# One indirect transfer for all experts' table entries, later loads of the sums' weights and tables, and products of constants at the start, in a conditioned mixture-of-experts layer

## The chip, the core and the metric

The kernel runs on one core of a Trainium2 chip. The metric is the device time in microseconds; the time before is the median of three runs. A profile is one further execution, taken with the hardware profiler, and its rows are in microseconds from the start of its span.

## The reference

For x of 8 x 256 x 1024 (2048 tokens), each of the 8 batches has its own 1024 x 1024 matrix, picked by a number in `itok`; its product with x is the input of a feed-forward layer, whose result is added to x. All in float32.

```
h      = einsum("bsi,boi->bso", x, weight[itok])
g, u   = split(h @ shared_w_gate_up.T);   shared = silu(g) * u @ shared_w_down.T
probs  = softmax(h @ gate_w.T);           two best of 16 experts, their weights scaled to sum 1
g, u   = split(h @ w_gate_up[e].T);       out_e  = silu(g) * u @ w_down[e].T
result = x + shared + sum over the two experts of weight * out_e
```

The condition matrices are loaded by an index that is known at run time alone, and so are the experts' rows.

## The kernel before

**Products in three parts.** Every float32 operand is split into a high part (a cast on ACT, L80) and a low part (a subtraction on DVE, L81), and each product is three matmuls (`mm3`, L103): high by high, high by low, low by high. `load_w` (L89) loads one tile of 128 x 1024 (512 KB) from SP's queue into one of 4 staging buffers `st`, and splits it into one of 5 buffers `hl`. A load can be issued only when the split that used its staging buffer is done; a split can begin only when PE has finished with its `hl` buffer.

**Work between loads.** `between` is a list of small works: `load_w` takes one after each of its splits and asks that it is issued after that split (`tc.issue_after`). Otherwise a planner, which estimates times, sets the order of each engine's instructions; `issue_after` holds a step back behind another. On each engine the instructions run in the order that results.

**Stages.** `cond(b)` computes the condition product of one batch: 8 tiles of weights `wc`, 2 tiles of `xT`, 96 matmuls of 128x512, and two stores of rows to `y_d`. `itok` comes by the very first transfer, and SP reads its number (L211) before it can issue a `wc` load. `route(g)` (L236) computes the gate for one of 4 groups of 512 tokens, picks the two experts on DVE, and writes each token's number and weight to `tab_d` by 8 indirect scatters from POOL (L333). `tab_d` has `SLOTS` places for each expert. `Up` computes the first shared matrices by a scheme of sums and differences of quarter matrices: `stage_a`, `stage_b`, `stage_c`, `stage_d`, each for units u = 0 to 3. `sums_b(u)` loads three tiles (`a11`, `a21` into spare places in `S` and `raw`, `a22` into a staging buffer), and DVE forms three sums of them (L443 to L445), which are split (`shl`), used, and stored in `ss_d` for the second half of the tokens; `sums_d(u)` loads two and forms one (L456). `shared_down(g)` is the second shared matrix, 8 tiles of `sd` for 512 tokens; DVE adds its results from PSUM into `acc` (L554), and SP stores them (L555). There are 7 PSUM banks that take turns.

**Order of the whole.** The main part (L725 to L761) interleaves the eight `cond` with `route` and the stages of `Up` for the first two groups. `tables` (L155) loads the gate's weights and fills `tab_d`; it stands in `between` for `cond(2)`. After `route(3)` a chain of small DVE operations (L778 to L817) sorts the experts by their number of tokens; `order` holds the expert at each place, and its capacity is from `CAPS`.

**Entries.** `entries(pool, ns)` (L660) reads the tables of the experts at places `ns`. For each it issues two transfers from SP, after reading the expert's number: `tb` (the same entries 32 to a row) and `cr` (one row an expert). `places` transposes `tb` on DVE (L676) and makes row numbers `ix` of them on POOL (`segments`, 4 instructions); `weights` transposes `cr`'s weights on PE (L683) and copies them to `cw`. It is called for places 0 and 1 before `shared_down(0)`, with `weights` in `between`, and for 2 to 15 before `shared_down(1)`, with both in `between`. `expert_rows(n)` gathers an expert's rows from `y_d` by 8 to 10 indirect transfers from POOL (L579), in 4 buffers `yg` and one `yl`, and DVE transposes them (L178). After `shared_down(1)` the 16 experts follow, then the shared part of the other two groups, and last `shared_down(2)` and `shared_down(3)`, which store to `out`.

Of the kernel before, what the change touches and what calls it, by code (L numbers as in the profile page):

```python
# [9 lines left out]
F32 = mybir.dt.float32  # L10
# [10 lines left out]
E, I, SI = 16, 256, 1024  # L21
NA = 8
NC = H // P
G = 4
GT = T // G
NB = GT // P

CAPS = (304, 296, 288, 288, 280, 280, 272, 272, 264, 264, 264, 256, 256, 256, 256, 256)
CAP = max(CAPS)
MAIN = 2 * P  # L30
SLOTS = T + CAP
ROW0 = [sum(CAPS[:n]) for n in range(E + 1)]
ZROW = ROW0[E]
PAD = 4 * T
# [3 lines left out]
def adapter_moe_kernel(ctx: ExitStack, tc: tile.TileContext, xT, x, itok, wc, gate, wgu, wd, sgu, sd, out):  # L38
# [43 lines left out]

    last_load = [None]

    homes, loads, last_gather, marks = [whl], [0], [None], []

    between = []

    def load_w(src, parts=1):  # L89
        st = wst.tile([P, 1024], F32, tag="wst", name="st")  # L90
        loads[0] += 1
        hl = homes[loads[0] % len(homes)].tile([P, 2, 1024], FR, tag="whl", name="hl")
        for i in range(parts):
            cs = slice(i * 1024 // parts, (i + 1) * 1024 // parts)
            last_load[0] = nc.sync.dma_start(st[:, cs], src[:, cs])
            end = split(hl[:, 0, cs], hl[:, 1, cs], st[:, cs])
        work = between.pop(0) if between else None
        if work:
            with tc.issue_after(end):
                work()  # L100
        return hl

    def mm3(ps, lhs, rhs, first, last):  # L103
        nc.tensor.matmul(ps, lhs[0], rhs[0], start=first, stop=False)  # L104
        nc.tensor.matmul(ps, lhs[0], rhs[1], start=False, stop=False)  # L105
        nc.tensor.matmul(ps, lhs[1], rhs[0], start=False, stop=last)  # L106


    cpool.tile([P, 96], F32, tag="cpad", name="cpad")
    at3 = [cpool.tile([P, 2, P], FR, tag=f"at3{k}", name=f"at3{k}") for k in range(2)]  # L110
    gpk = cpool.tile([P, NC * 2 * E + P], FR, tag="gpk", name="gpk")
    tri = cpool.tile([P, P], BF, tag="tri", name="tri")
    ones = cpool.tile([P, P], BF, tag="ones", name="ones")
    it_sb = cpool.tile([1, B], I32, tag="it_sb", name="it_sb")
    nc.sync.dma_start(it_sb, itok)

    ident = cpool.tile([2 * E, 2 * E], F32, tag="ident", name="ident")

# [13 lines left out]
    def constants(ring):  # L132
        make_identity(nc, ident)
        tri_f = ring.tile([P, 1024], F32, tag="op", name="tri_f")
        make_upper_triangular(nc, tri_f[:, :P], val=1.0, diag=False)
        nc.vector.tensor_copy(tri, tri_f[:, :P])
        nc.gpsimd.memset(ones, 1.0)
# [69 lines left out]
        split(yt[:, 0, :, off : off + n], yt[:, 1, :, off : off + n], tv[:, :, :n])  # L207

    def cond(b, rows):
        xt = [load_w(xT[b, :, 0, :], 2 if b == 0 else 1)]  # L210
        aid = nc.values_load(it_sb[0:1, b : b + 1], engines=(mybir.EngineType.SP,), min_val=0, max_val=NA - 1)  # L211
        yrow = [rows.tile([P, 1024], F32, tag="yrow", name=f"yrow{k}") for k in range(2)]
        for h in range(2):
            ps = [bank() for k in range(2)]
            for q in range(4):
                if h == 0 and q == 1:
                    xt.append(load_w(xT[b, :, 1, :]))
                w = load_w(wc[ds(aid, 1), h * 4 + q].rearrange("a p f -> p (a f)"), 2 if b == 0 and h == 0 and q == 0 else 1)
# [155 lines left out]
    class Up:  # L374
# [59 lines left out]
        def sums_b(self, u):  # L434
# [1 line left out]
                return load_w(ss_d[1, u]), load_w(ss_d[2, u])  # L436
            v = nc.vector.tensor_tensor
            a11, a21 = self.spare_b[u]
            nc.sync.dma_start(a11, sgu[0, 0, u])
            nc.sync.dma_start(a21, sgu[1, 0, u])  # L440
            a22 = wst.tile([P, 1024], F32, tag="wst", name="a22")
            nc.sync.dma_start(a22, sgu[1, 1, u])
            v(a11, a11, a21, op=ALU.subtract)  # L443
            v(a21, a21, a22, op=ALU.add)
            v(a22, a22, a11, op=ALU.subtract)  # L445
# [4 lines left out]
        def sums_d(self, u):  # L450
            if not self.first:
                return load_w(ss_d[0, u]), load_w(ss_d[3, u])
            s2, a12 = self.spare_d[u]
            nc.sync.dma_start(s2, ss_d[1, u])
            nc.sync.dma_start(a12, sgu[0, 1, u])
            nc.vector.tensor_tensor(a12, a12, s2, op=ALU.subtract)  # L456
            return load_w(ss_d[0, u]), self.made(3, u, a12)

# [74 lines left out]
    def shared_down(g, h, ring, acc, dst):  # L533
        ht = None
        ts = [slice(g * GT + k * P, g * GT + (k + 1) * P) for k in range(NB)]
        for n in range(2):
# [15 lines left out]
                        )  # L552
            for k in range(NB):
                nc.vector.tensor_tensor(acc[k][:, hs], ps[k], acc[k][:, hs], op=ALU.add)  # L554
                nc.sync.dma_start(dst[ts[k], hs], acc[k][:, hs])  # L555


    def combine(pool, tbs, base):
# [98 lines left out]

    def entries(pool, ns):  # L660
        n0, n1 = ns[0], ns[-1] + 1
        tb = pool.tile([32, E, 32, 2], I32, tag="tb", name="tb", bufs=1)
        cr = pool.tile([E, CAP, 2], F32, tag="cr", name="cr", bufs=1)
        ib = pool.tile([32, E, 32], F32, tag="ib", name="ib", bufs=1)
        nc.gpsimd.memset(tb[:, n0:n1], 0)
        nc.gpsimd.memset(cr, 0.0)
        for n in ns:
            e = expert_id(n)
            t = -(-CAPS[n] // 32)
            nc.sync.dma_start(tb[:t, n], tab_d[ds(e * SLOTS, 32 * t), :].rearrange("(t i) o -> t i o", i=32))  # L670
            nc.sync.dma_start(
                cr[n : n + 1, : CAPS[n], :].bitcast(I32), tab_d[ds(e * SLOTS, CAPS[n]), :].rearrange("(u r) o -> u r o", u=1)
            )

        def places():
            nc.vector.transpose(ib[:, n0:n1], tb[:, n0:n1, :, 0].bitcast(F32))  # L676
            segments(ix[:, n0:n1, :], ib[:, n0:n1, :10].bitcast(I32))

        def weights():
            ct = psm.tile([P, 3, E], F32, tag="sm", name="ct")  # L680
            for j in range(3):
                m = min(P, CAP - j * P)
                nc.tensor.transpose(ct[:m, j, :], cr[:, j * P : j * P + m, 1], ident[:E, :E])  # L683
            for j in range(3):
                m = min(P, CAP - j * P)
                nc.vector.tensor_copy(cw[:m, j, n0:n1], ct[:m, j, n0:n1])

        return places, weights

# [38 lines left out]
        constants(ring)  # L728
    up = Up(True, raw, X, S_, G, ring, ys, 0)
    w = up.rows_work(0)  # L730
    between[:] = [None, w[0], w[1], lambda: tables(ring), None, w[2], None, w[3]]
    cond(2, ys)
    up.begin()
    route(0, [(lambda c: chunk(up.b11 if c < 4 else up.b21, c % 4), GT)])
# [46 lines left out]
    order = once("order", [P, E], I32)  # L781
# [7 lines left out]
    v.tensor_tensor(sq, perm, by_col(rev1), op=ALU.mult)  # L789
    v.tensor_reduce(red, sq, axis=AX.X, op=ALU.add)  # L790
    v.tensor_scalar(order, red, -1.0, float(E), op0=ALU.mult, op1=ALU.add)
    v.tensor_tensor(sq, perm, by_row(caps[:, :]), op=ALU.mult)
    v.tensor_reduce(capof, sq.rearrange("p n e -> p e n"), axis=AX.X, op=ALU.add)

# [22 lines left out]
        v.tensor_scalar(si, row, float(ZROW), None, op0=ALU.add)  # L817
    pa = pool("pa", 1)
    pe = pool("pe", 1)
    places, weights = entries(pe[1], [0, 1])  # L820
    places()
    e0 = expert_rows(pa[1], 0)
    between[:] = [None] * 4 + [weights]
    shared_down(0, G, ring, down_rows(0, ys), xs_d)
    rs = expert_rows(pa[1], 1)
    places, weights = entries(pe[1], range(2, E))
    yt, works = expert_yt_work(pa[1], e0)
    between[:] = [works[0], None, works[1], places, works[2], None, weights]
# [156 lines left out]
```

## Time and profile before

| What | Value |
|---|---|
| Median of three runs | 1003.31 us (1002.62 to 1003.84) |
| The profiled execution's own time | 1005.67 us |
| Its span | 1003.8 us |
| Mean granted clock | 0.997 |
| First, last start of a matmul | 7.33 us, 997.13 us |
| HBM | 203.17 MB read, 48.25 MB written |

The page's chain of work that ended last, by engine and then by line (shares of the span; "issue" is time in which an engine waited for nothing that the profile shows):

```profile
PE 84%; DMA 6%; POOL 3%; issue 3%; DVE 2%; SPq 1%; ACT 1%; ACTq 0%; POOLq 0%; DVEq 0%
```

It says that PE sets the time nearly throughout, and that some 16% of the chain runs over other engines, mostly where PE was fed just in time. Its slices of the span (40 of 25.1 us) show where the transfers are heavy (DMA in tenths of 16 engines' time):

```profile
DVE  5567588565875886847978878878785324565531
DMA  8988647978768133739988888888878999956931
```

The first 100 us and 175 to 200 us are the stretches with the busiest DMA of the first half; at 325 to 350 us it is nearly idle. Busy shares are averages: what a wait costs is read from the timeline of the engine that waits.

### The profile page before, as it was taken

To read this page: it belongs to the slowest core of one execution; us is meant where nothing else is said; L and a number is where in the kernel's file an instruction comes from. 1 tells how busy PE (TensorE), PEld (TensorE's weight loads), DVE (VectorE), ACT (ScalarE), POOL (GpSimd) and SP (SyncE) were. 2 spreads that over 40 slices of the span, in tenths; PEclk is the share of its full clock that TensorE was granted. 3 is DMA by queue.
4 is the path that set the end of the run, shared out by engine and by line. 5 is a ranking of instruction groups with operands and counts; after the bars stand their busy time and mean duration, and the time that the engine had idled before them with its cause. 6 is when DMAs were issued, how large, how long until landed. Compare 5 with 4: busy or idle time off the path is not lost.

```text
span 1003.8 us, 14185 instructions
## 1 busy us (share of the span) xinstructions
PE 980.0 (98%) x5043; PEld 839.8 (84%) x5043; DVE 661.6 (66%) x886; ACT 531.6 (53%) x709; POOL 303.5 (30%) x312
## 2 busy tenths in 40 slices
PE   6989999999999999989999999999999999999997
PEld 5868888888788888869999999999998888888886
DVE  5567588565875886847978878878785324565531
ACT  5546466466563451316777767767665556233220
POOL 1000303000003004847885664650003442503200
PEclk9999999999999999999999999999999999999999
DMA  8988647978768133739988888888878999956931
GB/s 296 319 299 296 210 148 230 389 271 308 283 219 296 44 126 118 268 117 358 332 315 297 269 292 288 278 286 306 283 252 305 260 327 305 290 147 198 263 127 44
DMA packets 83782, 252.45 MB, mean 251 GB/s; under 512 B 13366, under 2 KB 22198, under 8 KB 83702
## 3 DMA queue, kind: packets, MB, share of 16 engines
q1 hardware_dynamic: 51526, 174.07, 50.5%
q0 software_dynamic: 19312, 60.47, 20.7%
q10 hardware_dynamic: 12864, 16.91, 4.6%
q8 instruction: 41, 0.67, 0.3%
q14 instruction: 39, 0.32, 0.1%
HBM read 203.17 MB, written 48.25 MB: 250 GB/s over the span
## 4 chain that ended last, share of the span: by engine, by line
PE 84%; DMA 6%; POOL 3%; issue 3%; DVE 2%; SPq 1%; ACT 1%; ACTq 0%; POOLq 0%; DVEq 0%
PE acc L425 28%; PE acc L105 18%; PE acc L106 18%; PE acc L104 17%; DMA st<-wc 3%; PE acc L647 2%; POOL yg L579 2%; DMA y_d<-yrow 1%; DMA yr<-y_d 1%; PE lp L242 1%; DVE hl L81 1%; POOL tab_d L333 1%; ACT hl L80 1%; DMA st<-xT 1%; SPq L670 0%
## 5 line engine op out<-in xcount | busy, mean ns | idle before, releaser
L81 DVE TENSOR_TENSOR hl<-st,hl 128x1024 fp32r<-128x1024 f32 (+1 forms) x254 | 305.0, 1209 | 176.8 <-ACT hl L80 175.7
L80 ACT CAST hl<-st 128x1024 fp32r<-128x1024 f32 (+1 forms) x254 | 262.9, 1042 | 203.6 <-PE acc L106 80.4
L425 PE MATMUL acc<-op,hl 128*128 128x512 f32 x1056 | 242.6, 390 | 0.5 <-DVE hl L81 0.5
L425 PEld LDWEIGHTS acc<-op,hl 128*128 128x128 f32 x1056 | 197.5, 188 | 41.7 <-DVE hl L81 1.0
L579 POOL DMA_INDIRECT yg<-y_d,ix x128 | 162.7, 1271 | 57.9 <-issue 34.1
L104 PE MATMUL acc<-yte,hl 128*128 128x256 f32 (+6 forms) x512 | 147.4, 288 | 0.0
L106 PE MATMUL acc<-yte,hl 128*128 128x256 f32 (+6 forms) x512 | 147.3, 288 | 0.0
L105 PE MATMUL acc<-yte,hl 128*128 128x256 f32 (+6 forms) x512 | 146.9, 287 | 0.0
L105 PE MATMUL acc<-hl 128*128 128x512 f32 x256 | 101.0, 394 | 2.8 <-DVE hl L81 2.8
L104 PE MATMUL acc<-hl,ht 128*128 128x512 f32 x256 | 99.6, 392 | 1.4 <-DVE acc L554 1.4
L105 PE MATMUL acc<-hl,ht 128*128 128x512 f32 x256 | 100.6, 393 | 0.0
L104 PE MATMUL acc<-hl 128*128 128x512 f32 x256 | 92.1, 395 | 8.6 <-ACT hl L80 8.6
L106 PE MATMUL acc<-hl 128*128 128x512 f32 x256 | 100.4, 392 | 0.0
L106 PE MATMUL acc<-hl,ht 128*128 128x512 f32 x256 | 100.0, 392 | 0.0
L105 PEld LDWEIGHTS acc<-yte,hl 128*128 128x128 f32 x512 | 96.4, 188 | 0.6
L104 PEld LDWEIGHTS acc<-yte,hl 128*128 128x128 f32 x512 | 96.4, 188 | 0.6
L106 PEld LDWEIGHTS acc<-yte,hl 128*128 128x128 f32 x512 | 96.2, 188 | 0.0
L347 POOL DMA_DIRECT2D yr<-y_d x24 | 13.3, 552 | 249.5 <-DMA y_d<-yrow 138.4
L425 PE MATMUL acc<-op,shl 128*128 128x512 f32 x288 | 66.7, 389 | 0.0
L104 PEld LDWEIGHTS acc<-hl 128*128 128x128 f32 x256 | 48.3, 190 | 19.4 <-ACT hl L80 9.5
L425 PEld LDWEIGHTS acc<-op,shl 128*128 128x128 f32 x288 | 54.1, 188 | 11.2
L333 POOL DMA_INDIRECT tab_d<-tid,sli x32 | 35.1, 1098 | 87.7 <-DVE ranks L326 78.9
(191 smaller groups left out, 1330.5 us busy)
## 6 DMA issues: line engine op xcount, KB each, us to landing
st<-wgu SPq DMA_DIRECT2D x64, 512.0 KB
st<-wc SPq DMA_DIRECT2D x63, 512.0 KB
st<-sd SPq DMA_DIRECT2D x32, 512.0 KB
st<-wd SPq DMA_DIRECT2D x32, 512.0 KB
os_d<-o SPq DMA_DIRECT2D x32, 512.0 KB
yr<-y_d POOLq DMA_DIRECT2D x24, 512.0 KB, 6.4
st<-sgu SPq DMA_DIRECT2D x24, 512.0 KB
st<-ss_d SPq DMA_DIRECT2D x20, 512.0 KB
```

Source lines behind the costliest of these rows:

```text
L80: nc.scalar.copy(hi, src)
L81: return nc.vector.tensor_tensor(lo, src, hi.bitcast(F32), op=ALU.subtract).ins
L104: nc.tensor.matmul(ps, lhs[0], rhs[0], start=first, stop=False)
L105: nc.tensor.matmul(ps, lhs[0], rhs[1], start=False, stop=False)
L106: nc.tensor.matmul(ps, lhs[1], rhs[0], start=False, stop=last)
L242: nc.tensor.matmul(lp[:, n0 : n0 + n], gpk[:, c * 2 * E : c * 2 * E + P], get(c)[l], start=(c == 0 and l == 0), stop=(c == NC - 1 and l == 1),
L333: i = nc.gpsimd.indirect_dma_start(out=tab_d[:, :], out_offset=bass.IndirectOffsetOnAxis(ap=sli[:, k : k + 1], axis=0), in_=tid[r][:, tb, ...
L347: nc.gpsimd.dma_start(r, y_d[tb].rearrange("a (i t) f -> (a i) (t f)", t=4))
L425: nc.tensor.matmul(ps, lhs[x], rhs[y], start=(first and c == 0 and i == 0), stop=(c == 3 and i == 2), skip_group_check=True)
L579: last_gather[0] = nc.gpsimd.indirect_dma_start(out=r[:, t * 256 : (t + 1) * 256], out_offset=None, in_=y_d.rearrange("k a p f -> (k a p) f"),
L647: nc.tensor.matmul(ps, a3[:, fi, :], w[fi][:, l, hs], start=(fi == 0 and l == 0), stop=(fi == 1 and l == 1))
```

## The change

Four groups of edits.

- **Entries.** `SLOTS` grows from 2352 to 2560, a multiple of `ENTRIES` = 320, so that `tab_d` can be read as rows of 320 entries. A new column of 16 numbers, `column`, holds the row of the expert at each place; three small DVE operations make it after `order`. `entries` is called once: it clears `cr` (now 32 x 320 x 2), fetches all 16 experts' rows by one indirect transfer from POOL, and transposes the numbers straight from `cr`. `tb` and its 16 transfers are gone, as are `cr`'s 16. `places` is called for 0 and 1, and for 2 to 15 after the gathers of the first expert in the text; in POOL's order both sets of `segments` stand ahead of the first gather. `weights` runs once for all experts, behind the last product issued so far.
- **Start.** `constants` no longer fills `ones`; a memset does so first, and 12 matmuls of `ones` by `ones` (128 x 512, bf16) write to a PSUM tile that nothing reads. `load_first` loads the first tile of x and the first of weights in halves: x, weights, weights, x; the second tile of x is loaded before the third tile of weights and not before the second.
- **Later loads.** The work `tables` is held behind the last load issued; so are the loads of `sums_b` and `sums_d`. In SP's order the gate and the filling of `tab_d` now come after the fourth load of `cond(2)`, where they stood among the loads of `cond(0)`. The loads of `sums_b` for units 0 and 1 (2 and 3) come after the last weights of `cond(4)` (`cond(5)`) in one row of six; the first two of unit 0 stood among the loads of `cond(0)`, the others between those of the blocks nearby. The loads of `sums_d` come after those of `cond(7)`.
- **End.** The last four stores of the last `shared_down` are issued by ACT.

```diff
-SLOTS = T + CAP
+ENTRIES = -(-CAP // 32) * 32
+SLOTS = -(-(T + CAP) // ENTRIES) * ENTRIES
...
+    def load_first(xsrc, wsrc):
+        pieces = []
+        for src in (xsrc, wsrc):
+            st = wst.tile([P, 1024], F32, tag="wst", name="st")
+            loads[0] += 1
+            pieces.append((src, st, homes[loads[0] % len(homes)].tile([P, 2, 1024], FR, tag="whl", name="hl")))
+        for k, i in ((0, 0), (1, 0), (1, 1), (0, 1)):
+            src, st, hl = pieces[k]
+            cs = slice(i * 512, i * 512 + 512)
+            with tc.issue_after(last_load[0].ins):
+                last_load[0] = nc.sync.dma_start(st[:, cs], src()[:, cs])
+            split(hl[:, 0, cs], hl[:, 1, cs], st[:, cs])
+        return pieces[0][2], pieces[1][2]
...
+    def after_loads(work):
+        def later():
+            with tc.issue_after(last_load[0].ins):
+                work()
+
+        return later
...
-        nc.tensor.matmul(ps, lhs[1], rhs[0], start=False, stop=last)
+        last_product[0] = nc.tensor.matmul(ps, lhs[1], rhs[0], start=False, stop=last).ins
...
+    nc.gpsimd.memset(ones, 1.0)
+    warm = psm.tile([P, 4, P], F32, tag="sm", name="warm")
+    for k in range(12):
+        nc.tensor.matmul(warm, ones, ones[:, :].rearrange("p (o n) -> p o n", o=1).to_broadcast([P, 4, P]), start=True, stop=True)
...
-                if h == 0 and q == 1:
+                if h == 0 and q == 2:
                     xt.append(load_w(xT[b, :, 1, :]))
...
-            nc.sync.dma_start(a11, sgu[0, 0, u])
-            nc.sync.dma_start(a21, sgu[1, 0, u])
+            with tc.issue_after(last_load[0].ins):
+                nc.sync.dma_start(a11, sgu[0, 0, u])
+                nc.sync.dma_start(a21, sgu[1, 0, u])
             a22 = wst.tile([P, 1024], F32, tag="wst", name="a22")
-            nc.sync.dma_start(a22, sgu[1, 1, u])
+            last_load[0] = nc.sync.dma_start(a22, sgu[1, 1, u])
...
-            nc.sync.dma_start(s2, ss_d[1, u])
-            nc.sync.dma_start(a12, sgu[0, 1, u])
+            with tc.issue_after(last_load[0].ins):
+                nc.sync.dma_start(s2, ss_d[1, u])
+                nc.sync.dma_start(a12, sgu[0, 1, u])
...
-                nc.sync.dma_start(dst[ts[k], hs], acc[k][:, hs])
+                (nc.scalar if g == GN - 1 and n else nc.sync).dma_start(dst[ts[k], hs], acc[k][:, hs])
...
+    def entries(pool, column):
+        cr = pool.tile([32, ENTRIES, 2], F32, tag="cr", name="cr", bufs=1)
+        ib = pool.tile([32, 10, 32], F32, tag="ib", name="ib", bufs=1)
         nc.gpsimd.memset(cr, 0.0)
...
+        nc.gpsimd.indirect_dma_start(
+            out=cr[:E, :, :].rearrange("e s o -> e (s o)").bitcast(I32),
+            out_offset=None,
+            in_=tab_d.rearrange("(e s) o -> e (s o)", s=ENTRIES),
+            in_offset=bass.IndirectOffsetOnAxis(ap=column, axis=0),
+        )
+        nc.vector.transpose(ib, cr[:, :, 0].rearrange("p (t i) -> p t i", i=32))
...
-    between[:] = [None, w[0], w[1], lambda: tables(ring), None, w[2], None, w[3]]
+    between[:] = [None, w[0], w[1], after_loads(lambda: tables(ring)), None, w[2], None, w[3]]
...
+    v.tensor_tensor(sq[:E, 0, :], red[:E, :], ident[:E, :E], op=ALU.mult)
+    v.tensor_reduce(red[:E, 0:1], sq[:E, 0, :], axis=AX.X, op=ALU.add)
+    v.tensor_scalar(column, red[:E, 0:1], -float(SLOTS // ENTRIES), float(SLOTS // ENTRIES * E), op0=ALU.mult, op1=ALU.add)
...
-    places, weights = entries(pe[1], [0, 1])
-    places()
+    places, weights = entries(pe[1], column)
+    places(0, 2)
     e0 = expert_rows(pa[1], 0)
+    places(2, E)
     between[:] = [None] * 4 + [weights]
     shared_down(0, G, ring, down_rows(0, ys), xs_d)
     rs = expert_rows(pa[1], 1)
-    places, weights = entries(pe[1], range(2, E))
     yt, works = expert_yt_work(pa[1], e0)
-    between[:] = [works[0], None, works[1], places, works[2], None, weights]
+    between[:] = [works[0], None, works[1], None, works[2]]
```

More of the change, by code (lines that the diff above doesn't have):

```diff
@@ L23 @@
 NC = H // P
-G = 4
-GT = T // G
+GN = 4
+GT = T // GN
 NB = GT // P
@@ L83, in adapter_moe_kernel, with load_w @@
     last_load = [None]
+    last_product = [None]
     homes, loads, last_gather, marks = [whl], [0], [None], []
     between = []
-    def load_w(src, parts=1):
+    def load_first(xsrc, wsrc):
[11 more added lines that the diff above has]
+        return pieces[0][2], pieces[1][2]
+    def load_w(src):
         st = wst.tile([P, 1024], F32, tag="wst", name="st")
@@ L92, in load_w @@
         hl = homes[loads[0] % len(homes)].tile([P, 2, 1024], FR, tag="whl", name="hl")
[L93 to L96, printed above, removed]
+        last_load[0] = nc.sync.dma_start(st, src)
+        end = split(hl[:, 0, :], hl[:, 1, :], st)
         work = between.pop(0) if between else None
@@ L105, in mm3 @@
         nc.tensor.matmul(ps, lhs[0], rhs[1], start=False, stop=False)
-        nc.tensor.matmul(ps, lhs[1], rhs[0], start=False, stop=last)
+        last_product[0] = nc.tensor.matmul(ps, lhs[1], rhs[0], start=False, stop=last).ins
     cpool.tile([P, 96], F32, tag="cpad", name="cpad")
     at3 = [cpool.tile([P, 2, P], FR, tag=f"at3{k}", name=f"at3{k}") for k in range(2)]
-    gpk = cpool.tile([P, NC * 2 * E + P], FR, tag="gpk", name="gpk")
+    gpk = cpool.tile([P, NC * 2 * E + P - 8], FR, tag="gpk", name="gpk")
     tri = cpool.tile([P, P], BF, tag="tri", name="tri")
@@ L114, in adapter_moe_kernel @@
     it_sb = cpool.tile([1, B], I32, tag="it_sb", name="it_sb")
-    nc.sync.dma_start(it_sb, itok)
+    last_load[0] = nc.sync.dma_start(it_sb, itok)
+    nc.gpsimd.memset(ones, 1.0)
+    warm = psm.tile([P, 4, P], F32, tag="sm", name="warm")
+    for k in range(12):
+        nc.tensor.matmul(warm, ones, ones[:, :].rearrange("p (o n) -> p o n", o=1).to_broadcast([P, 4, P]), start=True, stop=True)
     ident = cpool.tile([2 * E, 2 * E], F32, tag="ident", name="ident")
@@ L136, in constants @@
         nc.vector.tensor_copy(tri, tri_f[:, :P])
-        nc.gpsimd.memset(ones, 1.0)
         for r in range(2):
@@ L209, in cond, with weights @@
     def cond(b, rows):
-        xt = [load_w(xT[b, :, 0, :], 2 if b == 0 else 1)]
-        aid = nc.values_load(it_sb[0:1, b : b + 1], engines=(mybir.EngineType.SP,), min_val=0, max_val=NA - 1)
+        aid = []
+        def weights(k):
+            if not aid:
+                aid.append(nc.values_load(it_sb[0:1, b : b + 1], engines=(mybir.EngineType.SP,), min_val=0, max_val=NA - 1))
+            return wc[ds(aid[0], 1), k].rearrange("a p f -> p (a f)")
+        if b == 0:
+            x0, w0 = load_first(lambda: xT[b, :, 0, :], lambda: weights(0))
+            xt = [x0]
+        else:
+            xt, w0 = [load_w(xT[b, :, 0, :])], None
         yrow = [rows.tile([P, 1024], F32, tag="yrow", name=f"yrow{k}") for k in range(2)]
@@ L215, in cond @@
             for q in range(4):
-                if h == 0 and q == 1:
+                if h == 0 and q == 2:
                     xt.append(load_w(xT[b, :, 1, :]))
-                w = load_w(wc[ds(aid, 1), h * 4 + q].rearrange("a p f -> p (a f)"), 2 if b == 0 and h == 0 and q == 0 else 1)
+                w = w0 if w0 and h == q == 0 else load_w(weights(h * 4 + q))
                 for k in range(2):
@@ L656, in segments, with places @@
             nc.gpsimd.tensor_scalar(ix[32 * a : 32 * a + 32], ib, float(P * a), None, op0=ALU.add)
[L660 to L665, printed above, removed]
-        nc.gpsimd.memset(cr, 0.0)
[L667 to L677, printed above, removed]
+    def entries(pool, column):
+        cr = pool.tile([32, ENTRIES, 2], F32, tag="cr", name="cr", bufs=1)
+        ib = pool.tile([32, 10, 32], F32, tag="ib", name="ib", bufs=1)
+        nc.gpsimd.memset(cr, 0.0)
+        nc.gpsimd.indirect_dma_start(
[5 more added lines that the diff above has]
+        nc.vector.transpose(ib, cr[:, :, 0].rearrange("p (t i) -> p t i", i=32))
+        def places(n0, n1):
+            segments(ix[:, n0:n1, :], ib.rearrange("p t n -> p n t")[:, n0:n1, :].bitcast(I32))
@@ L679, in weights @@
         def weights():
             ct = psm.tile([P, 3, E], F32, tag="sm", name="ct")
+            with tc.issue_after(last_product[0]):
+                for j in range(3):
+                    m = min(P, CAP - j * P)
+                    nc.tensor.transpose(ct[:m, j, :], cr[:E, j * P : j * P + m, 1], ident[:E, :E])
             for j in range(3):
                 m = min(P, CAP - j * P)
[L683 to L686, printed above, removed]
+                nc.vector.tensor_copy(cw[:m, j, :], ct[:m, j, :])
@@ L780, in adapter_moe_kernel @@
     perm, red, capof = once("perm", [P, E, E], BF), once("red", [P, E]), once("capof", [P, E])
-    order = once("order", [P, E], I32)
+    order, column = once("order", [P, E], I32), once("column", [E, 1], I32)
     v.tensor_copy(cnt, cp)
```

## The prediction

> **What bounds the kernel now.** I read the page's first part, the busy time of the engines in stretches of 20 us, the waits of PE, and then the timelines of single engines at the places these name.
>
> ```profile
> PE 980.0 (98%) x5043; PEld 839.8 (84%) x5043; DVE 661.6 (66%) x886; ACT 531.6 (53%) x709; POOL 303.5 (30%) x312
> ```
>
> PE is the bound, but its busy share hides the losses: matmuls overlap, and a slow clock counts as busy. I therefore took the distance from the start of each matmul to the start of the next. With the clock at full rate a 128x512 product takes 227 ns. All products at the usual distance of their shape need 970.5 us. The first starts at 7.33 us, the last at 997.13, and the end of the span is 1003.8. So 7.3 us lie ahead, 6.7 behind, and 19.3 us are excess between. In stretches: 3.5 us of it in 0 to 20, 4.5 in 20 to 80, 0.4 in 80 to 120, 1.1 in 120 to 140, 2.0 in 260 to 280, 1.7 in 420 to 440 and 4.8 in 440 to 460; nearly nothing elsewhere. No change that leaves the products alone can win more than these. The stretches (us, PE busy and matmuls, granted clock, DMA share, GB/s):
>
> ```profile
> 0.00:20.00 20.00, 11.93 (x41) 1.00 0.83 286
> 180.00:200.00 20.00, 20.00 (x90) 1.00 1.01 396
> 420.00:440.00 20.00, 18.60 (x83) 1.00 0.50 184
> 440.00:460.00 20.00, 16.96 (x76) 0.91 0.77 266
> ```
>
> 90 products in 20 us is full speed. The waits of PE (us in total, times, longest; the 7.3 in the first row is the time ahead of the first product) name who ends the rest:
>
> ```profile
> PE acc L104 <- ACT hl L80: 8.6, 3, 7.3
> PE ct L683 <- DMA cr<-tab_d: 3.0, 1, 3.0
> PE acc L105 <- DVE hl L81: 2.8, 4, 1.4
> PE acc L104 <- DVE acc L554: 1.4, 1, 1.4
> ```
>
> **Part 1, the tables of entries.** PE's timeline around 440:
>
> ```profile
> 441.77 0.39 PE L104 MATMUL acc<-hl,ht 128*128 128x512 f32 x1
> 445.20 0.43 PE L683 MATMUL ct<-ident,cr 16*128 16x16 f32 x3 [3.04 <-DMA cr<-tab_d]
> 445.56 0.79 PE L105 MATMUL acc<-hl,ht 128*128 128x512 f32 x1
> 448.71 0.40 PE L106 MATMUL acc<-hl,ht 128*128 128x512 f32 x1
> ```
>
> PE stands still for the transposes of `cr`, and then starts a product only every 0.43 us up to 448.71: the clock has halved. SP's own timeline says why `cr` is late, for these are the first and the last of 27 transfers issued one by one:
>
> ```profile
> 431.80 0.29 SPq L671 DMA_DIRECT2D cr<-tab_d  x1
> 443.82 0.23 SPq L671 DMA_DIRECT2D cr<-tab_d  x1
> ```
>
> The first waits until POOL, busy with gathers of rows, has cleared `cr` (7.0 us in SP's waits), the others cost 12 us of issue. Excess here: 3.2 us of stall and 1.6 of slow clock. The 1.6 before it, at 433.03, is DVE: it stands at transposes of gathered rows while the copy that frees a PSUM bank (L554) is queued behind them:
>
> ```profile
> 432.94 1.25 DVE L178 STREAM_TRANSPOSE tt<-yg 128x1024 f32<-128x1024 f32 x1 [0.56 <-DMA yg<-y_d,ix]
> 434.11 0.65 DVE L554 TENSOR_TENSOR acc<-acc,acc 128x512 f32<-128x512 f32 x1
> ```
>
> The change takes away all 32 transfers and brings `cr` whole by one indirect transfer from POOL. It waits for the last scatter into `tab_d`, landed at 396.5. The near row is such a scatter, 2.2 us from issue to landing (384.02 to 386.20), or the first gather, 2.9 (401.94 to 404.79): `cr` is there at 398.8 to 399.5, where the first `tb` now comes at 399.1. The three small DVE operations for `column` (some 0.2 us each) come before 394 and are hidden by the scatters. The transposes of `cr` stand 6 products earlier in PE's order than the first set now (401.23), near 399.9, so 0 to 1 us of wait there. POOL's order grows ahead of the first gather:
>
> ```profile
> 399.45 1.42 POOL L656 TENSOR_SCALAR ix<-ib 32x20 int32<-32x20 int32 x4 [4.80 <-DVE ib L676]
> 400.93 0.84 POOL L665 MEMSET tb<- 32x896 int32 x1
> 401.94 1.05 POOL L579 DMA_INDIRECT yg<-y_d,ix  x1 [0.17 <-POOL tb L665]
> ```
>
> The memset goes, and the four wide segments, 2.41 us at 445.56, come in: gathers start 1.7 to 2.5 us later. All of experts 0 and 1 then land near 438; those of expert 2 follow at once and not from 448 on. DVE's new order has the first L554 ahead of the second `tt` of expert 1, where it is behind it now, but still behind the first, so it ends near 433.4 and about 0 to 1.5 us of the stall at 433 stay. Sum: 6.4 us of excess, 1.0 left, **gain 5.4** (bounds 2 and 6.4). What is late next is the rows of expert 2 (445 at 1.55 us a gather), behind which DVE holds weights that PE wants at 449.
>
> **Part 2, the start.** PE's first products:
>
> ```profile
> 7.33 1.22 PE L104 MATMUL acc<-hl 128*128 128x512 f32 x2 [7.33 <-ACT hl L80]
> 11.76 0.42 PE L105 MATMUL acc<-hl 128*128 128x512 f32 x1
> 12.61 0.73 PE L104 MATMUL acc<-hl 128*128 128x512 f32 x2 [0.21 <-ACT hl L80]
> ```
>
> They start 0.43 us apart until 11.76, although the record of the granted clock says 1.00. Twelve products of ones start after POOL's first memset, near 1.0, and last 4.9 to 5.2 us; they delay nothing, since no operand is there. By the row, PE needs 4.4 us of work to get its clock, which the twelve just give, and ten products at half rate cost 2.1 us. The Trainium skill (TensorE: Matmul & The Clock Gate, The HAM clock gate) has it that a window of about 3.4 us of activity releases the clock: 1.7 us. The same page loses the clock after an idle window of 3.4 us, yet here 3.04 us sufficed at 442; so I count no more than 3 us of idle as safe, and between the twelve and the first operand there is about 1. Neither 2.1 nor 1.7 is the gain, for the operands bound this stage: the next weights (cast at 11.51 to 12.6) start PE again at 12.61. In the new order half a tile less lies ahead of the first weights (0.5 us earlier) and half a megabyte less ahead of the second, which by the 264 GB/s between the casts at 6.66 and 11.51 gives 11.3 in place of 12.61. But the third weights now wait for a staging buffer until about 9.5, where they were issued at 6.49, and give most of that back. I take **1.0** (bounds 0 and 2.1).
>
> **Part 3, loads moved later.** Gate (64 KB), the table's first filling (294 KB, now 320), and for unit 0 of the sums two loads of 512 KB and a store of 512 KB leave the first 25 us: about 1.9 MB, or 6 us at 310 GB/s, ahead of the loads PE waits for up to 71 us. The tables come back at about 50 us. Of the 4.5 us in 20 to 80, 0.5 (at 35.6) should go; 1.9 at 57 to 60 and 1.5 at 71 hang on the round trip of `y_d` (6.4 us out, 6.4 back), and at 71 DVE now splits one more weight tile ahead of the transpose it waits in. **Gain 2.0** (bounds 0 and 4.5).
>
> Against it: the sums' three loads of units 0 and 2 now come after the last weights of the fifth and sixth condition block. Behind L443 and L444, which wait for them, DVE holds the last two splits of those weights and then the splits of the sums themselves. Last weight issued at 161.91; two loads at 162.3 and 162.7, `a22` at 164.3 for its buffer as now. Landing takes 6.0 us (163.04 to 169.01) to 8.6 (180.05 to 188.66, at a DMA share of 1.01): sums split by 177 to 179, and PE wants them at 178; for unit 2 221 against 222.5. So 0 to 2 us at either, **cost 1.0** (bounds 0 and 4). Units 1 and 3 have 11 us more, and the last stage's loads move into 293 to 350, where the DMA is half idle.
>
> **Part 4, the end.** Four stores go to ACT's queue. SP issues them 1.36 us apart, each when DVE is done, so it queues nothing: 0 (bounds -0.4 and 0.4). The Trainium skill (DMA: Bandwidth & Descriptors, Issuing engines are not separate DMA queues) allows at most the saved issue time: 0.33 us for one store.
>
> **Sum.** 5.4 + 1.0 + 2.0 - 1.0 = 7.4 us. The profiled execution took 1005.67 with a span of 1003.8: 998.3 and 996.4 after. The median of the runs is 1003.31, so **995.9 us**.
>
> **Rivals.**
> A, only one half works: the gathers start late enough that DVE holds bank or weights at 433 or 449 for over 3 us and the clock falls again. Part 1 gives 2; 1003.3 - 4.0 = 999.3. For it: DVE is already late there by its gathers, and 2 us come on top. Against it: the bank's copy moves ahead. Chance 0.2.
> B, the whole excess goes: 6.4 + 2.1 + 4 - 0 gives 990.8. Chance 0.1.
> C, slower: the late sums. If their loads take 12 us under the tab scatters and stores, PE waits 5 us at units 0 and 2 and restarts each time at half clock (1.6): -13.2 + 8.4 = 4.8 slower, 1008. It decides from about 10 us of landing time; 8.6 is the longest row I found. Chance 0.08.
> D, no effect within 0.2% (2 us, what a measurement here can tell): the new waits eat the gains. Chance 0.06; 1003.
> My own case 0.56, 993 to 998.5. The range holds it, A and B: 990.5 to 1001. Faster 0.86, same 0.06, slower 0.08.
>
> **What would show it.** Right: no L671, PE excess in 420 to 460 under 2 us, first real products 0.23 us apart and near 6.8. Wrong: a wait of PE on `ct` or on L554 over 2 us, half-rate products after 440, or PE waiting for `shl` near 175 and 218.

## The result, and the profile after

The changed kernel is slower: a median of 1010.98 us (1009.18 to 1014.89, six runs) beside 1002.73 for the kernel before (six runs on the same chip), a ratio of 1.0089 with a 95% interval of 1.0066 to 1.0111. All ratios in this document compare fast runs with fast runs; the profiles of e5, e6 and e10 are of slow ones. The profiled execution took 1010.49 us with a span of 1008.7. PE's row of the page has the same share as before, now with the twelve products of constants in it:

```profile
PE 986.6 (98%) x5052; PEld 842.4 (84%) x5052; DVE 660.6 (65%) x885; ACT 531.0 (53%) x709; POOL 309.5 (31%) x310
```

The stretches of 20 us of the changed kernel (us, PE busy and matmuls, granted clock, DMA share, GB/s) show where it lost:

```profile
0.00:20.00 20.00, 15.93 (x59) 1.00 0.78 244
60.00:80.00 20.00, 20.00 (x89) 1.00 0.70 242
80.00:100.00 20.00, 18.54 (x82) 1.00 0.93 338
120.00:140.00 20.00, 17.78 (x92) 1.00 0.33 79
160.00:180.00 20.00, 18.34 (x79) 1.00 0.93 229
400.00:420.00 20.00, 17.97 (x74) 0.91 0.29 87
420.00:440.00 20.00, 17.89 (x72) 0.91 0.98 348
440.00:460.00 20.00, 20.00 (x90) 1.00 0.81 273
```

From 20 to 80 us PE now runs full, and at 440 the old stall is gone. New losses stand at 80 to 100, 120 to 140, 160 to 180, and 400 to 440. Its waits (us in total, times, longest) give them names:

```profile
PE acc L127 <- ACT hl L82: 3.5, 3, 1.5
PE acc L462 <- DVE shl L83: 2.9, 1, 2.9
PE acc L127 <- DVE acc L593: 2.1, 1, 2.1
PE ct L721 <- DMA cr<-tab_d,column: 2.0, 1, 2.0
PE acc L462 <- ACT X L503: 1.5, 1, 1.5
```

By starts of products, the excess over the usual distance went from 4.5 to 0.3 us in 20 to 80; from 0.4 to 2.5 in 80 to 120; from 1.1 to 3.5 in 120 to 140; from 0 to 5.6 in 160 to 200 (the wait for `shl` at 178, then products at half rate, 0.43 us apart); and from 6.7 to 7.9 in 400 to 460. So in this pair of profiles PE won 1.2 us up to 20 us (with the time ahead of its first product) and 4.2 in 20 to 80, and lost 2.1 in 80 to 120, 7.9 in 120 to 200 and 1.2 in 400 to 460: the largest loss lies far ahead of the place where the entries are read. VectorE's timeline gives the cause of the wait for `shl`: it stands for two loads of unit 1, issued at 163.62 and 164.41, with the split that PE wants behind it.

```profile
179.05 1.22 DVE L481 TENSOR_TENSOR raw<-raw 128x1024 f32<-128x1024 f32 x1 [2.88 <-DMA raw<-sgu]
180.19 1.22 DVE L83 TENSOR_TENSOR shl<-a,shl 128x1024 fp32r<-128x1024 f32 x1
```

In 400 to 440 two short stalls took the place of the two of before, each followed by slow products; PE's timeline at the first:

```profile
406.36 0.43 PE L721 MATMUL ct<-ident,cr 16*128 16x16 f32 x3 [2.03 <-DMA cr<-tab_d,column]
...
408.05 0.63 PE L127 MATMUL acc<-hl,ht 128*128 128x512 f32 x1
408.48 0.63 PE L128 MATMUL acc<-hl,ht 128*128 128x512 f32 x1
```

and POOL's timeline says why `cr` and the gathers are late:

```profile
398.07 0.97 POOL L370 DMA_INDIRECT tab_d<-tid,sli  x1 [0.30 <-issue]
403.75 0.88 POOL L705 DMA_INDIRECT cr<-tab_d,column  x1 [4.71 <-DMA tab_d<-tid,sli]
406.92 5.50 POOL L695 TENSOR_SCALAR ix<-ib 32x20 int32<-32x20 int32 x8 [2.29 <-DVE nbf L841]
412.59 1.56 POOL L618 DMA_INDIRECT yg<-y_d,ix  x1 [0.17 <-POOL ix L695]
```

The one transfer landed 2.5 us after its issue, as forecast. But it waited 4.7 us for the last scatter to land; before, the first table read stood 2.9 us behind the last scatter, here 5.7. The list of DMA issues (names, operation, count, median us to landing) has the scatters of the kernel before and of the changed kernel, in this order:

```profile
tab_d<-tid,sli POOLq DMA_INDIRECT x32, 4.6
tab_d<-tid,sli POOLq DMA_INDIRECT x32, 6.5
```

Either trace holds the landing of 28 of the 32. In each of the four groups of tokens they land later: medians of 3.5, 5.2, 6.6 and 2.9 us before, of 5.3, 7.3, 9.4 and 5.8 in the changed kernel. That is one key to the result, and the trace alone does not say what in the change made it.

### The profile page after: what moved, and what is told of

It reads as the page before. It is cut to its first block, busy times and chain, and to the rows that moved or that the text cites. A ratio compares the mean times of both kernels' runs of the same rounds, so it can differ in the third digit from the quotient of the medians.

```text
span 1008.7 us, 14045 instructions
## 1 busy us (share of the span) xinstructions
PE 986.6 (98%) x5052; PEld 842.4 (84%) x5052; DVE 660.6 (65%) x885; ACT 531.0 (53%) x709; POOL 309.5 (31%) x310
## 4 chain that ended last, share of the span: by engine, by line
PE 85%; DMA 7%; POOL 2%; DVE 2%; ACT 1%; issue 1%; SPq 0%; ACTq 0%; POOLq 0%; DVEq 0%
PE acc L462 28%; PE acc L128 18%; PE acc L129 18%; PE acc L127 18%; PE acc L686 2%; DMA raw<-sgu 1%; DMA st<-wc 1%; DMA y_d<-yrow 1%; POOL tab_d L370 1%; DVE hl L83 1%; DMA yg<-y_d,ix 1%; ACT hl L82 1%; DMA yr<-y_d 1%; PE lp L279 1%; POOL ix L695 0%
## 5 line engine op out<-in xcount | busy, mean ns | idle before, releaser
L618 POOL DMA_INDIRECT yg<-y_d,ix x128 | 160.2, 1252 | 58.7 <-issue 33.8
```

Source lines behind the costliest of these rows:

```text
L618: last_gather[0] = nc.gpsimd.indirect_dma_start(out=r[:, t * 256 : (t + 1) * 256], out_offset=None, in_=y_d.rearrange("k a p f -> (k a p) f"),
```

## Experiments

All ratios are to the kernel before, run beside each on the same chip. E5 to e12, e17 and e18 fell on chips where every kernel, the kernel before among them, took some 25 us longer. Their profiles show this loss behind 430 us: 9.6 to 22.0 us of PE's excess in 440 to 480 (20.1 in e6, the kernel before but for an unused end of `tab_d`; 4.8 in the kernel before itself), the rest later. Its cause is not known. Of these runs only ratios and mostly the stretches ahead of 430 are used; where a ratio may hang on what comes later, it is said. Their traces hold no landings of scatters.

**First round: which part costs it?** At this point I held the late loads of the sums to be the main cause (theory S).

**e1**, the changed kernel with the sums' loads as before:

```diff
-            with tc.issue_after(last_load[0].ins):
-                nc.sync.dma_start(a11, sgu[0, 0, u])
+            nc.sync.dma_start(a11, sgu[0, 0, u])
...
-            last_load[0] = nc.sync.dma_start(a22, sgu[1, 1, u])
+            nc.sync.dma_start(a22, sgu[1, 1, u])
```

> The changed kernel with the loads of the sums issued as in the kernel before (no order after the last load, s2/a12/a11/a21/a22 early); all other parts of the change stay. Theory S (the late loads of the sums made the product at 178 us wait 2.9 us for shl and lost the clock behind it): the stall and the half-rate products in 160-200 us go, 5.6 us less, 1005-1006 us, ratio to before 1.002-1.004. Rival D (the stretch 160-200 is crowded by other parts of the change, the scatters of the tables' entries and y_d stores, whichever loads come when): a stall of 2-3 us stays there, 1009-1011 us.

Measured: 1.0090 (1.0065 to 1.0114). The wait for `shl` is gone, but another of 1.7 us stands at 174.6. The excess in 160 to 200 fell from 5.6 to 1.9 us in the profile, other stretches lost as much, and the time is the same. Theory S fell.

**e2**, the reverse: the kernel before with the sums' loads late and nothing else.

> The kernel before with the later loads of the sums alone. Theory S: a PE wait on shl of 2-3 us at unit 0 and half clock behind it, 5 us more than before, 1007-1008.5 us. My prediction's step (cost of late sums 1.0 us, part of a gain of 2.0 in 20-80 us): 1001-1003.5 us. Rival D: 1002-1003 us, no wait on shl above 1 us, since only all parts together crowd the stretch.

Measured: 0.9997 (0.9985 to 1.0008), no wait for `shl`. The late loads cost nothing by themselves.

**e3**, the kernel before with the edits of `SLOTS`, `ENTRIES`, `column` and `entries` alone.

> The kernel before with the one indirect transfer of the table entries alone (new slots, column, entries, ct after a product). My prediction: 5.4 us less than before, 997-998 us. Theory E (the transfer waits for the last scatter, ct stands too early in PE's order and the gathers come later, so that two stalls with half clock replace two): excess of 400-460 us 7-8 us against 6.7, 1003-1005 us. If the lateness of the scatters' landing (5.6 us after issue in the changed kernel against 2.8 before) comes from the other parts, ct waits under 1 us here and the time is 999-1001 us.

Measured: 1.0099 (1.0076 to 1.0121), 1012.19 us. This part alone makes a loss as large as that of the whole change (some 2 us of it behind the last product: 8.7 us in its profile, where the kernel before has 6.7 and the changed kernel, with its last stores on ACT, 6.3). Its list of DMA issues has the slow scatters too:

```profile
tab_d<-tid,sli POOLq DMA_INDIRECT x32, 6.1
```

and it lost time where the edited code does not run at all: in 160 to 180 us, where PE had been full. The stretch before and in e3:

```profile
160.00:180.00 20.00, 20.00 (x90) 16.55 (x89) 15.83 (x15) 11.76 (x15) 7.26 (x7) 1.00 0.90 288
160.00:180.00 20.00, 18.69 (x81) 14.79 (x80) 14.27 (x13) 9.91 (x13) 6.34 (x7) 1.00 0.99 232
```

(after the busy time of the five engines come clock, DMA share, GB/s). The DMA engines are busy for 0.99 of the stretch and move 232 GB/s; in the kernel before they moved 288 at a share of 0.90. What the edit changes there is where the scatters write: an expert's list is 2,560 places long and not 2,352.

**e4**, the kernel before with the new start and the later tables.

> The kernel before with the first loads in new order, the products of constants and the later table loads alone. My prediction gives 1.0 us for the start and at most 2.0 us for the loads in 20-80 us: 1000-1001.5 us. Theory R (the lead of 5.5 us that the changed kernel has at 80 us is given back by 140 us because X, ACT and the y_d round trip hold the product at 124 us): PE's excess is 5 us lower to 80 us and 3-4.5 us higher in 80-140 us, 1001-1002.5 us. Rival (the loss in 80-140 comes of the other parts): the lead holds, 997-998.5 us.

Measured: 1.0018 (1.0004 to 1.0033). Not a gain but a loss.

**Second round: the length of the lists (theory A).**

**e5, e10, e17**: the kernel before with one number changed.

```diff
-SLOTS = T + CAP
+SLOTS = 2560
```

> The kernel before with one number changed: an expert's list in tab_d has 2,560 places (20,480 bytes, five times 4,096) in place of 2,352 (18,816 bytes); entries are read as before. Theory A (lists that begin at equal places modulo 4,096 bytes make the scatters of 128 entries slower): the scatters land after 6-7 us on average in place of 4.7-4.9, and part of the 9 us of the entries alone comes with it, 1006-1009 us. Theory E (the loss is all in the transfer and its order: ct early, gathers late): scatters as before, 1002-1004 us.

> The kernel before with lists of 2,560 places, again, beside 2,568 and 4,096 on one chip. Theory A: scatters land 1.3-2.3 us later than with 2,568, ratio to before 1.003-1.009. Rival P2: as 2,568.

> The kernel before with lists of 2,560 places. Theory A: scatters land after 6-7 us on average, 3-6 us slower than before, ratio 1.003-1.006. Rival P2 (size): equal to 2,568 places. If the ratio is 0.998-1.002 while the scatters are late, their lateness matters only together with the one transfer.

Measured: 1.0064 (1.0027 to 1.0102), 1.0028 (0.9995 to 1.0061) and 1.0028 (1.0000 to 1.0056): 3 to 6 us slower by the middle values. The first is clear of noise; the other two point the same way, but their intervals reach down to no loss.

**e6**: `tab_d` allocated at the larger size, lists of 2,352 places.

> The kernel before with tab_d allocated at the changed kernel's size, so that os_d, xs_d and ss_d lie where they do there, but with lists of 2,352 places as before. Theory A: no change, scatters 4.7-4.9 us, 1002-1004 us. Rival P (it is the place of the buffers behind tab_d that matters, not the lists): as e5, 1006-1009 us.

Measured: 1.0001 (0.9962 to 1.0039). The interval would leave room for the 0.28% of e10 and e17, but PE is full in 160 to 180 us, as in the kernel before: no sign that it is the place of the buffers behind the table.

**e9, e18**: `SLOTS = 2568`.

> The kernel before with lists of 2,568 places (20,544 bytes, 64 more than five times 4,096), a size within 0.4% of the changed kernel's. Theory A (equal starts modulo 4,096): scatters as before, about 4.8 us to landing, no change, ratio 0.998-1.002. Rival P2 (it is the size of the table, not where its lists begin): as with 2,560 places, scatters 6-7 us, ratio 1.004-1.009.

> The kernel before with lists of 2,568 places. Theory A: scatters 4.7-5 us, ratio 0.999-1.001. Rival P2: as 2,560 places.

Measured: 1.0012 (0.9980 to 1.0044) and 1.0054 (1.0015 to 1.0093). The first interval holds both no loss and the 0.28% of e10 and e17, the second shows a loss; in the table below e9 stands at the edge of the profiles with 2,560 places, e18 among them. Equal starts modulo 4,096 bytes, as I had put theory A, are neither shown nor excluded by these two runs.

**e11**: `SLOTS = 4096`.

> The kernel before with lists of 4,096 places (32,768 bytes, eight times 4,096). Theory A: at least as slow as 2,560 places, since the lists begin at equal places modulo 32,768 too: scatters 6-9 us, ratio 1.004-1.015. Rival P2 (size): worse than 2,560 in the same way, so this run tells nothing between the two alone; a ratio under 1.002 would speak against both.

Measured: 1.0143 (1.0102 to 1.0185), the largest loss of a single number.

The intervals of 2,560 and 2,568 are wide, but the stretch of 160 to 180 us separates 2,352 from 2,560 places in all profiles but one, that of e15. DMA share and GB/s there:

| Places in a list | Profiles | DMA share | GB/s | PE busy of 20 us |
|---|---|---|---|---|
| 2352 | before, e2, e4, e6, e7, e8, e12, e13, e14, e16 | 0.84 to 1.00 | 285 to 361 | 20.00 |
| 2352 | e15 | 0.84 | 253 | 19.45 |
| 2560 | changed, e1, e3, e5, e10, e17 | 0.93 to 0.99 | 220 to 280 | 18.34 to 19.77 |
| 2568 | e9, e18 | 0.92 to 0.96 | 246 to 282 | 18.14 to 19.88 |
| 4096 | e11 | 0.99 | 225 | 17.74 |

PE's excess in 120 to 200 us, a stretch with scatters and no reading of the tables, separates them in every profile: 1.0 to 2.6 us in the eleven with 2,352 places, 3.3 to 9.2 in the six with 2,560, 7.2 in e11, and 2.1 and 4.9 in e9 and e18. E13 and e14 are among the eleven: they read the entries in the new way, on a chip without the later loss, and their scatters land after a median of 5.6 and 4.5 us. So the slow stretch goes with the length of the lists and not with the one transfer.

**e7 and e8**: the changed kernel, and the entries alone, with lists of the old length. Pieces of 336 entries still let one transfer find each list.

```diff
-ENTRIES = -(-CAP // 32) * 32
+ENTRIES = 336
...
-        nc.vector.transpose(ib, cr[:, :, 0].rearrange("p (t i) -> p t i", i=32))
+        nc.vector.transpose(ib, cr[:, :320, 0].rearrange("p (t i) -> p t i", i=32))
```

> The changed kernel with pieces of 336 entries in place of 320, so that a list is 7 of them, 2,352 places, as before the change; one indirect transfer still reads all experts' entries. Theory A: scatters land after 4.7-5 us, the wait of the transfer for the last of them goes from 4.7 to about 2 us, and the loss in 120-180 us goes too: 1002-1006 us. Theory E: no change, 1009.5-1012 us.

> The kernel before with the one indirect transfer alone, in pieces of 336 entries (lists of 2,352 places). Against 1012.2 us with pieces of 320. Theory A: 1000-1005 us; by my prediction's working without the slower scatters 998 us; what remains above 1002.7 is the price of ct's early place and the later gathers (theory E's share). Theory E: 1010-1013 us.

Measured: 1.0001 (0.9972 to 1.0029) against 1.0089, and 1.0014 (0.9990 to 1.0037) against 1.0099. These two ratios show no loss, but they can't be taken for the length of the lists alone: in 430 to 480 us, where these chips lose time anyway, PE lost 18 us in either profile and 24 in e6's, and this may have hidden a loss ahead of it. What the profiles show ahead of 430 is that the loss in 120 to 200 is gone (2.2 and 1.5 us, where the changed kernel has 9.2 and e3 4.8), and that PE no longer waits for `ct`, since in e7 the one transfer is issued 3.4 us behind the last scatter. In 400 to 430, however, e7 still loses 6.7 us, as much as the kernel before in 400 to 460: with the old lists too, no gain appears. POOL's and VectorE's timelines of e7 show what holds it:

```profile
399.20 0.88 POOL L705 DMA_INDIRECT cr<-tab_d,column  x1 [2.47 <-DVE pos L848]
402.38 5.54 POOL L695 TENSOR_SCALAR ix<-ib 32x20 int32<-32x20 int32 x8 [2.30 <-DVE nbf L841]
408.09 1.56 POOL L618 DMA_INDIRECT yg<-y_d,ix  x1 [0.17 <-POOL ix L695]
```

```profile
414.72 0.16 DVE L856 TENSOR_TENSOR row<-row,ranks 128x16 f32<-128x16 f32 x1
419.97 1.25 DVE L205 STREAM_TRANSPOSE tt<-yg 128x1024 f32<-128x1024 f32 x1 [5.09 <-DMA yg<-y_d,ix]
421.14 1.85 DVE L593 TENSOR_TENSOR acc<-acc,acc 128x512 f32<-128x512 f32 x3
```

VectorE stands 5.1 us for the first gathered block, and the three additions that free PE's banks (L593) are queued behind. PE lost 3.9 us at 418.

**Third round: the order of the entries' steps, and the start.**

**e12**: e7 with the wide segments behind the gathers of experts 0 and 1.

```diff
-    places(2, E)
...
     rs = expert_rows(pa[1], 1)
+    with tc.issue_after(last_gather[0].ins):
+        places(2, E)
```

> The changed kernel with pieces of 336 entries (lists of 2,352 places), and the segments of experts 2 to 15 issued on POOL behind the gathers of experts 0 and 1 in place of ahead of them. Theory: POOL's 4.1 us of wide segments are what puts the first gathers at 408 in place of 404, so VectorE's first transposition of a gathered block waits 5 us with three additions of L593 behind it, and PE loses 3.9 us at 418; with the segments behind, that stall falls to 0-1 us: 4 us less than the changed kernel with 336, ratio to before 0.994-0.998. Rival: other work takes the place of the stall (DMAs of the gathers among the loads of sd), ratio 0.998-1.002.

Measured: 0.9918 (0.9886 to 0.9951). The ratio can't be taken for the theory: the gathers did start 3.5 us earlier, but VectorE still stood 5.9 us, the one transfer came 5.9 us behind the last scatter (this wait varies from run to run with the old list too), `ct` waited for it (2.4 us at 399.6), and PE's excess in 380 to 440 was 10.0 us. The gain lies in 440 to 480, where these chips lose time anyway (12.9 us in its profile, 20.1 in e6's).

**e13**: further, the transpositions of the gathered blocks behind all additions of the first `shared_down`, and `ct` in the second.

```diff
-    between[:] = [None] * 4 + [weights]
...
-    between[:] = [works[0], None, works[1], None, works[2]]
+    between[:] = [after_adds(works[0]), None, after_adds(works[1]), weights, after_adds(works[2])]
```

**e14**: the same without the new start and the later tables.

> The changed kernel with lists of 2,352 places, segments of experts 2 to 15 behind the first gathers, the transpositions of expert 0's gathered blocks behind all additions of the first shared_down, and ct in the second shared_down. Theory: with the waits of the additions gone, no bank stall at 415-430 and none on ct: excess of 400-460 us under 2 us, against 10 in e12 and 6.7 before: ratio to before 0.986-0.994. Rival: the transpositions, now late, hold up expert 0's first product at 450 us by 2-5 us: 0.994-1.000.

> The same order with lists of 2,352 places, but without the new start and with the tables loaded as before (the entries, the later sums and the last stores by ACT alone). If theory R holds (the start's lead is given back by 135 us) it is as fast as e13 or up to 0.2% faster; if the start's lead counts after all, e13 is 0.2-0.4% faster.

Measured: e13 0.9981 (0.9963 to 0.9998); e14 0.9956 (0.9935 to 0.9977), a median of 999.29 us beside 1003.05 on the same chip: faster than both kernels. In e13 the stretches behind the tables are full:

```profile
400.00:420.00 20.00, 20.00 (x90) 1.00 0.60 195
420.00:440.00 20.00, 20.00 (x90) 1.00 0.86 318
440.00:460.00 20.00, 20.00 (x111) 1.00 0.83 268
```

PE's excess in 400 to 460 is 0.2 us (0.9 in e14), where it was 6.7 before. The mechanism of the forecast works once lists and order are right; part of the rest of e13's expected gain went at the start (11.1 us of excess up to 120 us, 7.6 in e14).

**e15 and e16**: the kernel before with the new start alone, and with the later tables alone.

> The kernel before with the new order of the first loads and the products of constants alone. Prediction's part 2: 1.0 us less, ratio 0.999. Theory R (to 100 us the loads set the pace, PE's lead of 3 us is waited away): ratio 0.999-1.001, first route's copy of lp 2-3 us earlier, the second's at most 1 us. Rival (the products of constants cost the clock or the start): ratio 1.001-1.003.

> The kernel before with the loads of gate and tab_d's first contents behind the third conditioned block's loads alone. Prediction's part 3: up to 2.0 us less. Theory R: ratio 0.999-1.001. Rival (the first scatters have to wait for the later table, or its 300 KB fall beside loads that PE waits for): 1.001-1.003, with PE's excess higher in 80-140 us.

Measured: 1.0024 (1.0010 to 1.0039) and 0.9995 (0.9980 to 1.0010). The tables do nothing. The start costs 2.4 us. ACT's timeline of e15 shows how the pieces of the first operands come in,

```profile
4.19 0.62 ACT L80 CAST hl<-st 128x512 fp32r<-128x512 f32 x1 [2.15 <-DMA st<-xT]
...
6.18 1.23 ACT L80 CAST hl<-st 128x512 fp32r<-128x512 f32 x2 [1.17 <-DMA st<-wc]
9.55 0.62 ACT L80 CAST hl<-st 128x512 fp32r<-128x512 f32 x1 [2.14 <-DMA st<-xT]
11.87 1.04 ACT L80 CAST hl<-st 128x1024 fp32r<-128x1024 f32 x1 [1.70 <-DMA st<-wc]
```

and PE's timeline what it does with them:

```profile
6.85 0.73 PE L117 MATMUL acc<-hl 128*128 128x512 f32 x2 [1.10 <-ACT hl L80]
...
12.97 0.73 PE L117 MATMUL acc<-hl 128*128 128x512 f32 x2 [2.83 <-ACT hl L80]
...
16.09 0.63 PE L119 MATMUL acc<-hl 128*128 128x512 f32 x1
16.52 0.63 PE L117 MATMUL acc<-hl 128*128 128x512 f32 x1
```

PE runs at the full rate from 6.85, is through the first pieces by 9.8 and stands 3.0 us for the next weights: the work that went twice as fast was waited for. And behind this stall the products are 0.43 us apart again: the profile's granted clock is 0.50 from 15.3 to 18.7 us, which costs 1.8. This is the rule and not the exception among the seven profiles with the new start. In e7, e12, e13 and e15 the granted clock fell for 3.4 us behind the stall near 10 us, which added 2.0 to 3.0; in e1 and e4 the first operand came 2.6 and 2.9 us after the constants, and the clock had fallen for 3.4 and 6.8 us by the first products (8.31 and 8.02 us). Only the changed kernel's own profile, with a stall of 1.7, kept it. A measure over all profiles is how late PE is against its products at their usual distance, constants left out. At 10 us of work it was 10.6 to 11.4 us late in six profiles with the old start and 2,352 places (before, e2, e6, e8, e14, e16), and 9.6 to 12.8 in seven with the new one (changed, e1, e4, e7, e12, e13, e15). At 130 us of work the means are 15.3 and 17.7.

## Why the prediction was wrong

I forecast 995.9 us, 7.4 less than before; the result is 8 more, outside the range. Two steps failed above all: the longer lists were priced at their bytes alone, and in part 1 the gathers and VectorE's place in the order were priced too low.

- **Part 1, its first input, and the growth of `SLOTS`.** "The last scatter into `tab_d`, landed at 396.5" was taken over from the kernel before; in the changed kernel it landed at 402.9, since it was issued 4.4 us later and took 4.8 us in place of 2.8. (The landing of the transfer itself, 2.2 to 2.9 us by the near rows, was right: 2.5.) The growth of `SLOTS` to 2560 was counted as bytes only, "294 KB, now 320". The runs show it as a cause of the loss. The scatters take a median of 6.1 to 6.8 us to land in the three traces that hold it (changed, e1, e3), in place of 4.3 to 5.6 in seven with the old list, and later in each of the four groups (the last: 5.3 to 6.3 in place of 2.8 to 4.5). One number costs 3 to 6 us alone (e5, with e10 and e17 at the edge of noise), and PE loses 3.3 to 9.2 us in 120 to 200 with 2,560 places against 1.0 to 2.6 with 2,352. That the whole of the loss comes of it is not shown, as e7 and e8 ran only on the chips with the later loss. A page of the Trainium skill (DMA: Bandwidth & Descriptors, Latency and other measured facts) speaks of copies that slow down at row pitches of large powers of two, where a pad of 192 bytes does not help and one of 4 KB does. Its case is another, pieces of 16 KB at pitches of 512 KB to 8 MB, and no run here isolates such a cause; but a pitch that the change moves was worth a line in the sum, and a bound in the range.
- **The wait on `ct`, "0 to 1 us".** 2.0 us, with half-rate products behind it. The place in PE's order was right, the time of `cr` wrong by the scatters; in e7 PE did not wait. But such a wait is not the long lists' alone: with the old ones, e12 waited too, 2.4 us.
- **Part 1, gathers "1.7 to 2.5 us later", stall at L554 "0 to 1.5" (gain 5.4).** This step takes away the gain even where the lists are as before. The wide segments took 4.1 of the 5.5 us in POOL's row, where I had priced them at 2.41; e7's gathers started at 408.1 (the changed kernel's at 412.6) in place of 401.9, VectorE stood 5.1 us for the first block with L593 behind it, and PE lost 3.9 us there and 6.7 in all, where I had left 1.0. In the changed kernel the stall at L593 was 2.1 us. With the order mended, e13 and e14 lose 0.2 and 0.9. I had named this as rival A, from the right mechanism, and sized it too small.
- **Part 2, the start (gain 1.0).** The sign was wrong: 2.4 us slower alone. In the changed kernel the full rate came (products 0.23 us apart from 6.58) and stayed, but in the six other profiles with this start it was lost again at once, behind waits of 2.6 and 2.9 us for the first operand or behind stalls of 2.0 to 3.0 for the next weights; "no more than 3 us of idle" was not safe. (The granted clock of 1.00 in the row for 0 to 20 us of the kernel before, at which the prediction wonders, is no measurement of its first products: the trace's record of the clock begins at 11.8 us.) And I let the loads bound only the next weights, not the pace of the whole first stage. Why PE is later still at 130 us, and whether the later second tile of x is to blame, was not tried apart.
- **Part 3 (gain 2.0, cost 1.0).** Both terms were near zero: 0.9995 for the tables, 0.9997 for the sums. What 20 to 80 us gained in the profile was lost again by 140: PE waited for weights at 87 (issued at 79.05, landed at 87.4) and at 124 for ACT, held by rows of `y_d`. Rival C's stall came, at unit 0: two loads landed some 15 us after issue, where 6.0 to 8.6 had been assumed and rival C wanted over 10, but only together with the slow scatters (e2, e7 and e13 have the late loads and no such wait).
- **Part 4, the end (0).** 6.3 us lie behind the last product in place of 6.7, at the edge of its bounds of 0.4.

The rivals held no version in which a step whose code was not edited got slower. The signs I had named came: a wait on `ct`, on L593, and for `shl` at 178.

Open: which property of the longer lists slows the scatters. 2,352 places are free of it, 2,560 and 4,096 are not. 2,568 (e18) speaks against exact multiples of 4,096 bytes as the condition, but e9 shows little, and its lists begin only 64 bytes apart modulo 4,096, so a near coincidence is not excluded, nor is the size of the table. Open too: how the 8 us divide between the lists and the order of steps, for want of e7 and e8 on a chip without the later loss.

## What to carry to other kernels

When a change alters a layout so that it can be read more simply, price the writers into it anew: their landing times from the old trace no longer hold, and all transfers beside them can slow with them. A buffer that is read one step earlier is worth nothing while an in-order engine ahead of it (POOL's segments, VectorE's transposition) waits with the freeing of PE's banks queued behind; order decided some 6 us here (PE's excess in 400 to 430: 6.7 in e7, 0.2 in e13), the one transfer by itself showed no gain. And an engine made faster in a stage that is fed just in time gets only to its next wait.

## What was not expected of the hardware

- Scatters of 128 entries of 8 bytes landed after a median of 4.3 to 5.6 us with lists 18,816 bytes apart and of 6.1 to 6.8 with lists 20,480 bytes apart; beside them, at a DMA share of 0.93 to 0.99, the whole core moved 220 to 280 GB/s in place of 285 to 361 (253 in one profile).
- The clock halved for less than the 3 us of idle that I had counted as safe. Such a loss lasted 3.4 us at a granted 0.50 (407.4 to 410.8 and 427.9 to 431.3 in the changed kernel), once, at e4's start, 6.8. In the changed kernel an excess of 2.2 us at 403.9 was enough, and in e13 one of 1.2 at 90.9; in e3 one of 2.6 at 402.8 left it at full rate. Over the ten traces without the later loss, up to 460 us, stalls that added between 1.2 and 2.95 us went either way, and all longer ones were followed by slower products. A short stall is to be priced with and without the 1.7 us of slow products that followed at 403.9.
